# Memory attention with a third buffer of weighed memories and shorter GpSimd steps, and the bias of the ternary layer added by VectorE tile by tile

## The chip, the cores and the metric

The kernel runs on one core of a Trainium2 chip. The time is the device time of one execution in microseconds, and a version is judged by the median of its runs. Engines are called PE (TensorE), PEld (its weight loads), DVE (VectorE), ACT (ScalarE) and POOL (GpSimd), as the profile calls them. Each engine works through its own queue in order; semaphores tie the queues together.

## The reference, cut to what matters

The input x has 8 sequences of 1024 positions with 256 channels. Six residual layers follow one another, each on a layer norm of x:

```python
x = x + 0.5 * fp4_ffn(ln(x))          # block-quantized, hidden 704
x = x + decay_attention(ln(x))        # 16 heads, a scan with a decaying state
x = x + 0.5 * fp4_ffn(ln(x))
x = x + 0.5 * ternary_ffn(ln(x))      # hidden 1024, biases b1 and b2
x = x + memory_attention(ln(x))       # 16 heads of 16
x = x + 0.5 * ternary_ffn(ln(x))
```

The change touches the last three. The ternary layer is `gelu(h @ W1.T + b1) @ W2.T + b2` with weights rounded to -1, 0 and 1. The memory attention is, per head,

```python
q, k, v = h @ Wq.T, h @ Wk.T, h @ Wv.T
sq, sk = elu(q) + 1, elu(k) + 1
rel   = sq . memory_norms[m]                       # for each of 4 memories m
mem   = sum_m softmax_m(mean_s rel) * (sq @ memories[m]) / max(rel, 1e-6)
num   = sq @ cumsum(sk (x) v);  den = max(sq . cumsum(sk), 1e-6)
out   = sigmoid(gate) * mem + (1 - sigmoid(gate)) * num / den
y     = concat_heads(out) @ Wo.T
```

## The kernel before

x stays in SBUF all the time, as 16 groups `X[g]` of 4 tiles of 128 positions x 256 channels (128 x 1024 numbers in fp32 per group, 64 tiles in all). The six layers are stages that run one after another; the statistics of the next layer norm and its first normalized group are begun inside the stage before (`begin`, `ln.advance`).

**The order of the queues.** `pin` chains an instruction behind the last pinned one of the same engine, so in the memory attention PE and DVE run in the order of the source text. POOL's and most of ACT's instructions are not pinned; the scheduler of the build puts them in their queues. In the ternary stages `loose` is set and the scheduler orders DVE too.

**Ternary stages** (`ffn_ternary`). Turn g of the loop transposes group g (`norm_turn`), multiplies group g-1 by W1 in eight chunks (`hidden`, 8 x 4 matmuls, then Gelu `hf`, a rounded copy `hh` on ACT and the rest `hl = hf - hh` on DVE, L1013), and multiplies group g-2 by W2 (`down`, 64 matmuls into `po`, added to x by DVE at L1035). At the start of `hidden`, POOL adds half of b2 to the whole group in one instruction of 128 x 1024 (L991).

**Memory attention** (`attn_memory`). An opening (`i == 0`) projects two groups and a quarter of the third (`project`, then `elu` on DVE, L1423), forms the running sums of sk (`running_sum`, a DVE scan, L1438; there is one buffer `kc` for each half of the channels), and takes the divisors of the first two groups (`divisors`: matmuls into `pr`, ACT copy to `rt`, POOL clamp at L1467). The next groups are normalized by ACT in two steps (L303, L311), tile by tile. After that iteration i works on four tiles at once, j = i mod 4:

- tile a = i-1: scores (`scored`, PE), `weigh_one` (DVE, L1079, 128 x 512), the state and the factors `rw` (DVE reciprocal of `psd` at L1718, product with the mixing weights `mw` at L1719);
- tile b = i-2: memory products `pmo` (PE), `weigh_memory` (DVE writes `mo`, L1586, four times 128 x 256 from PSUM), then `py` (PE, L1136 and L1154);
- tile c = i-3: `pn` (PE transposes), `y = pn * rw` (DVE, L1744), then four POOL additions of the four memories of `mo` into y (L1751);
- tile d = i-4: `pyt` (PE transposes of y), copied by ACT; tile e = i-5: `po` with wo, added to x by DVE (L1773).

The tile `mo` of 128 x 4 x 2 x 4 x 32 has two buffers, so `mo` of tile b cannot be written before the four additions of tile b-2 are done. `py` shares a PSUM bank with the first quarter of `pmo`, so PE begins `py` after the first `weigh_memory`. DVE's order in one iteration is:

```python
weigh_memory(0); weigh_one(1); weigh_memory(1..3)   # L1586, L1079
running_sum                                        # L1438, every second iteration
ln.advance; rw                                     # L1718, L1719
y                                                  # L1744
weigh_one(2), weigh_one(3), weigh_one(0)           # L1079
x += po; elu                                       # L1773, L1423
```

In iterations with j = 3 PE also runs `divisors` of a group two ahead, and POOL clamps its `rt`, 96 x 512 numbers. In the last 12 iterations nothing is projected any more. Once in 8 iterations a sequence begins, and the mixing weights (`mixing`, a softmax over the memories) are formed on the way: `pl` on PE, `lg` on DVE, and so on.

Of the kernel before, what the change touches and what calls it, by code (L numbers as in the profile page):

```python
# [9 lines left out]
F32 = mybir.dt.float32  # L10
# [7 lines left out]
P = 128  # L18
# [4 lines left out]
G = 4  # L23
# [15 lines left out]
def macaron_kernel(  # L39
# [906 lines left out]
    def ffn_ternary(last, after=None):  # L946
        with ExitStack() as st:
# [10 lines left out]
            def norm(g):  # L958
# [9 lines left out]
                xns[g] = xn  # L968

            def norm_turn(g):  # L970
                xn = xns.pop(g)
                xh = lnp.tile([P, 2, TG], F32R, tag="xh", name="xh")
                xl = lnp.tile([P, 2, TG], F32R, tag="xl", name="xl")
                for k in range(2):
                    pt = ps_t.tile([P, TG], F32, tag="pt", name="pt")
                    for j in range(G):
                        nc.tensor.transpose(
                            pt[:, j * P : (j + 1) * P], xn[:, j, k * P : (k + 1) * P], ident
                        )
                    nc.scalar.copy(xh[:, k, :], pt)  # L980
                    pin(
                        nc.vector.tensor_tensor(
                            xl[:, k, :], pt, xh[:, k, :].bitcast(F32), ALU.subtract
                        )
                    )
                xts[g] = (xh, xl)

            def hidden(g, between):

                pin(  # L990
                    nc.gpsimd.tensor_tensor(  # L991
                        X[g], X[g], b2h[:, None, :].to_broadcast([P, G, D]), ALU.add
                    )
                )
                xh, xl = xts.pop(g)
                hh = hp.tile([P, NF, TG], F32R, tag="hh", name="hh")
                hl = hp.tile([P, NF, TG], F32R, tag="hl", name="hl")
                for f in range(NF):
# [18 lines left out]
                    if f < len(between):  # L1017
                        between[f]()
                hs[g] = (hh, hl)

# [344 lines left out]
    def attn_memory(after):  # L1365
        with ExitStack() as st:
# [81 lines left out]
            def divisors(g, pr):  # L1448
# [17 lines left out]
                nc.scalar.activation(rt, pr[0 : NR + 32, :], AF.Identity, accum_out=su)  # L1466
                nc.gpsimd.tensor_scalar(rt, rt, EPS, 1.0, ALU.max, ALU.mult)  # L1467
                sums[g] = su
                proj[g] = (xt, sq, sk, rt)

            def weigh(b):
# [15 lines left out]
                def turned(pl):  # L1487
                    pin(
                        nc.tensor.matmul(pl, lhsT=sb, rhs=ident[:NR, :NR], start=True, stop=True)
                    )  # L1490
                    pin(nc.vector.tensor_scalar(lg, pl, 1.0 / S, None, ALU.mult))

# [100 lines left out]

            n = NG * G
            held = {}
            for i in range(n + 5):
# [3 lines left out]
                if i == 0:  # L1600

                    waiting = []
                    for u in range(min(GB + 1, NG)):
                        norm_turn(u, (2, 3), False)
                        if u < GB and u + 1 < NG:
                            xns[u + 1] = xn_pool.tile([P, G, D], F32, tag="xn", name="xn")
                        for v in range(G if u < GB else 1):
                            pp = ps_s.tile([P, TG], F32, tag="sc", name="pq" if v % 2 else "pk")
                            waiting.append((project(u, v // 2, v % 2 == 1, pp), u, v))
                            if u < GB and u + 1 < NG:  # L1610
                                ln.normalize(xns[u + 1], u + 1, v)
                            if len(waiting) > 1 or u == GB:
                                elu, *at_ = waiting.pop(0)
                                elu()
                                if at_[1] % 2 == 0:
                                    running_sum(at_[0], at_[1] // 2)
                        if u:
                            if waiting and waiting[0][1] == u - 1:
                                waiting.pop(0)[0]()
                            divisors(u - 1, bank(0, [P, TG], "pr"))  # L1620
                    for elu, *at_ in waiting:
# [5 lines left out]
                    if NG == GB:  # L1627
                        divisors(NG - 1, bank(0, [P, TG], "pr"))

# [5 lines left out]
                if 0 <= b < n:  # L1635
                    vz_b, ats_b, before_b, rw_b = chunk[b]
                    mo = cp.tile([P, 4, 2, NM, 2 * HD], F32, tag="mo", name="mo")

# [27 lines left out]
                for r in (1, 2, 3):  # L1666
                    weigh_memory(r)

                if 0 <= b < n:
# [16 lines left out]
                if divide:  # L1686
                    divisors(t, bank(3, [P, TG], "pr"))

# [52 lines left out]
                if 0 <= c < n:  # L1741
# [7 lines left out]
                    yv = y.rearrange("p (c r e) i -> p c r (e i)", c=2, e=2)  # L1749
                    for m in range(NM):  # L1750
                        nc.gpsimd.tensor_tensor(  # L1751
                            yv, yv, mo_c[:, :, :, m, :].rearrange("p r c n -> p c r n"), ALU.add
                        )
                    ys[c] = y
                weigh_one(2)
                weigh_one(3)
                last = t + 1 if j == 3 else t
                elu = None
                if i < n and last < NG:
                    m, of_q = (j + 1) % 4 // 2, j % 2 == 0  # L1760
                    elu = project(last, m, of_q, bank(2, [P, TG], "pq" if of_q else "pk"))
                    if not of_q:
                        held["sum"] = (last, m)
                weigh_one(0)
                if 0 <= a < n:
                    chunk[a] = (vz, [ats[r] for r in range(4)], before, rw)

                def output():
# [3 lines left out]
                    xe = X[e // G][:, e % G, :]  # L1772
                    pin(nc.vector.tensor_tensor(xe, po, xe, ALU.add))  # L1773


                if elu and 0 <= e < n:
                    output()
                if i < n and i % CB == 0:
                    mixing[1](bank(0, [P, NR], "pl"))
                if i < n and j == 2 and t + 1 < NG:  # L1780
# [5 lines left out]
                elif 0 <= e < n:  # L1786
                    output()
                if i < n and i % CB == 0:
# [64 lines left out]
```

## Time and profile before

| | us |
|---|---|
| median of 3 runs | 2725.47 (2719.73 to 2725.5) |
| the profiled execution | 2724.19 |
| its span, from the first to the last instruction | 2722.5 |
| PE busy | 2597.9 (95%) |
| DVE busy | 2088.3 (77%) |
| ACT busy | 1344.6 (49%) |
| POOL busy | 906.4 (33%) |
| L1013, DVE `hl`, 256 times | 210.9 |
| L991, POOL bias, 32 times | 78.3 |
| L1751, POOL additions into y, 256 times | 186.6 |
| L1586, DVE `mo`, 256 times | 95.8 |
| L1467, POOL clamp, 16 times | 31.6 |

The first ternary stage lies between about 1575 and 1847 us of the span, the memory attention between 1847 and 2455 us (its opening to 1880 us, its drain from 2441 us), the second ternary stage from there to the end. A line of the timeline gives the start, the time taken, the engine, the source line, the operation, what it writes and reads, the shape and the count; in square brackets stands how long the engine had been idle, and what released it. Instructions of one line that follow each other are drawn together, and the first and the last then span the time given. A busy share is an average over stages with different limits.

### The profile page before, as it was taken

Reading aid. Unit: us, or ns where it says so; the run is one execution under the profiler, and the core shown is the slowest. Engines: PE = TensorE matmul, PEld = TensorE weight load, DVE = VectorE, ACT = ScalarE, POOL = GpSimd, SP = SyncE. Lnnn points to the kernel's source line nnn. Section 1 sums busy time; section 2 is a strip of 40 time slices with the busy share of each in tenths; the row PEclk is TensorE's granted clock in tenths of the full one; section 3 lists DMA queues with packets and bytes.
Section 4 is the critical chain, followed back from the end, with each engine's and each line's share of the span. In section 5 each row is a group of like instructions: output and inputs, shape, how many; then the busy total and the mean of one; then the engine's idle time right before and its main releaser. Section 6 shows DMA issues by size and latency. Waiting matters only on the chain.

```text
span 2722.5 us, 52848 instructions
## 1 busy us (share of the span) xinstructions
PE 2597.9 (95%) x21270; PEld 1957.1 (72%) x21270; DVE 2088.3 (77%) x4669; ACT 1344.6 (49%) x2932; POOL 906.4 (33%) x817
## 2 busy tenths in 40 slices
PE   5899999999999998999999989999999999989999
PEld 3677777766666666777777778995666666667898
DVE  7888888858777678787878789755888877879775
ACT  5444444443333333444444456666555555436665
POOL 5444445421101003444444421102444444441110
PEclk9999999999999999999999999999999999999999
DMA  6000000000000000000000000000000000000011
GB/s 194 16 1 16 1 1 1 1 1 2 2 2 2 2 2 1 1 1 1 1 1 1 1 1 1 1 1 1 2 2 2 2 2 2 2 2 16 32 39 40
DMA packets 25877, 27.00 MB, mean 10 GB/s; under 512 B 4736, under 2 KB 24736, under 8 KB 25632
## 3 DMA queue, kind: packets, MB, share of 16 engines
q1 hardware_dynamic: 24688, 22.43, 2.6%
q8 instruction: 167, 2.74, 0.4%
q0 software_dynamic: 240, 0.54, 0.1%
q14 instruction: 78, 0.64, 0.1%
q10 hardware_dynamic: 704, 0.66, 0.1%
HBM read 15.23 MB, written 8.39 MB: 9 GB/s over the span
## 4 chain that ended last, share of the span: by engine, by line
PE 70%; DVE 16%; POOL 7%; issue 3%; ACT 2%; DMA 1%; SPq 0%; ACTq 0%; POOLq 0%; DVEq 0%
PE po L839 11%; PE pu L801 9%; PE pg L801 9%; PE po L1027 7%; PE ph L1002 7%; POOL y L1751 5%; PE py L1154 4%; PE sc L1070 3%; PE pk L1168 3%; PE pq L1168 3%; PE po L1168 3%; PE pkv L1168 3%; DVE hl L1013 2%; DVE ln_s L232 2%; PE py L1136 2%
## 5 line engine op out<-in xcount | busy, mean ns | idle before, releaser
L839 PE MATMUL po<-wd,ht 128*128 128x256 f32 (+1 forms) x1536 | 356.7, 382 | 6.1 <-DVE x L848 6.0
L801 PE MATMUL pg<-wgu,xt 128*128 128x352 f32 x1024 | 346.6, 460 | 8.8 <-ACT sg L812 8.6
L801 PE MATMUL pu<-wgu,xt 128*128 128x352 f32 x1024 | 347.3, 462 | 3.0 <-DVE h L814 3.0
L839 PEld LDWEIGHTS po<-wd,ht 128*128 128x128 f32 (+1 forms) x1536 | 283.7, 191 | 44.3 <-DVE x L848 9.0
L772 POOL TENSOR_TENSOR h<-h,q_sc 128x704 f32<-128x704 f32 x128 | 177.6, 1387 | 374.8 <-DVE h L769 370.9
L812 ACT ACTIVATE sg<-pg 128x352 f32<-128x352 f32 x256 | 117.8, 460 | 319.9 <-PE pg L801 319.6
L801 PEld LDWEIGHTS pu<-wgu,xt 128*128 128x128 f32 x1024 | 192.8, 191 | 106.8 <-DVE h L814 5.0
L801 PEld LDWEIGHTS pg<-wgu,xt 128*128 128x128 f32 x1024 | 193.8, 190 | 100.6 <-ACT sg L812 11.9
L1027 PE MATMUL po<-w,hh 128*128 128x256 f32 x1024 | 244.9, 281 | 9.1 <-DVE x L1035 9.1
L1027 PE MATMUL po<-w,hl 128*128 128x256 f32 x1024 | 245.1, 281 | 5.1 <-DVE hl L1013 5.1
L769 DVE SCALAR_TENSOR_TENSOR h<-qp,h 128x704 f32<-128x704 f32 x256 | 227.2, 887 | 20.0 <-ACT qp L765 15.5
L1013 DVE TENSOR_TENSOR hl<-hf,hh 128x512 fp32r<-128x512 f32 x256 | 210.9, 856 | 37.6 <-ACT hh L1011 34.0
L814 DVE TENSOR_TENSOR h<-sg,pu 128x352 f32<-128x352 f32 x256 | 129.5, 515 | 138.3 <-PE pu L801 103.5
L1751 POOL TENSOR_TENSOR y<-y,mo 128x256 f32<-128x256 f32 x256 | 186.6, 729 | 106.9 <-DVE y L1744 91.9
L1002 PE MATMUL ph<-xh,w 128*128 128x512 f32 x512 | 206.5, 405 | 0.9 <-DVE x L1773 0.5
L1002 PE MATMUL ph<-xl,w 128*128 128x512 f32 x512 | 204.3, 400 | 0.0
L991 POOL TENSOR_TENSOR x<-x,b2h 128x1024 f32<-128x1024 f32 x32 | 78.3, 2446 | 375.4 <-DVE xn L963 344.3
L1027 PEld LDWEIGHTS po<-w,hh 128*128 128x128 f32 x1024 | 192.9, 188 | 13.1 <-DVE x L1035 10.8
L758 POOL TENSOR_TENSOR h<-h,q_rs 128x704 f32<-128x704 f32 x128 | 177.7, 1388 | 71.3 <-DVE q_rs L754 59.3
L1027 PEld LDWEIGHTS po<-w,hl 128*128 128x128 f32 x1024 | 193.1, 189 | 7.7 <-DVE hl L1013 5.5
L1010 ACT ACTIVATE hf<-ph,b1c 128x512 f32<-128x512 f32 x256 | 168.5, 695 | 26.0 <-PE ph L1002 17.7
L1079 DVE TENSOR_TENSOR at<-sc,dec 128x512 f32<-128x512 f32 x256 | 158.5, 681 | 17.2 <-PE sc L1070 17.1
(248 smaller groups left out, 5571.4 us busy)
## 6 DMA issues: line engine op xcount, KB each, us to landing
x<-in_x SPq DMA_DIRECT2D x15, 512.0 KB, 8.9
out<-x SPq DMA_DIRECT2D x15, 512.0 KB, 2.9
raw_w<-in_w_t SPq DMA_DIRECT2D x2, 1024.0 KB, 5.3
wqkv<-in_wqkv_t SPq DMA_DIRECT2D x1, 768.0 KB, 6.3
wd_n<-in_w_down SPq DMA_DIRECT2D x1, 704.0 KB, 7.3
w_n<-in_w_up ACTq DMA_DIRECT2D x2, 256.0 KB, 6.6
w_n<-in_w_gate SPq DMA_DIRECT2D x2, 256.0 KB, 5.5
x<-in_x POOLq DMA_DIRECT2D x1, 512.0 KB, 6.0
```

The lines of the kernel that those rows point to most:

```text
L758: nc.gpsimd.tensor_tensor(vb, vb, rs[:, :, None].to_broadcast([P, nb, 16]), ALU.mult)
L769: pin(nc.vector.scalar_tensor_tensor(v, mg, FP4_LEAST, v, ALU.max, op))
L772: nc.gpsimd.tensor_tensor(vb, vb, sc[:, :, None].to_broadcast(list(vb.shape)), ALU.mult)
L801: nc.tensor.matmul(ps, lhsT=xts[g][:, k, j * P : (j + 1) * P], rhs=wgu[:, k, (2 * q + of_up) * NHALF : (2 * q + of_up + 1) * NHALF], start ...
L839: nc.tensor.matmul(po, lhsT=ht[:kn, c, :], rhs=wd[:kn, c, :], start=(c == 0), stop=(c == len(DCH) - 1),)
L1002: nc.tensor.matmul(ph, lhsT=w1[:, k, f * P : (f + 1) * P], rhs=xt[:, k, :], start=(k == 0 and xt is xh), stop=(k == 1 and xt is xl),)
L1010: nc.scalar.activation(hf, ph, AF.Gelu, bias=b1c[:, f : f + 1])
L1013: nc.vector.tensor_tensor(hl[:, f, :], hf, hh[:, f, :].bitcast(F32), ALU.subtract)
L1027: nc.tensor.matmul(po, lhsT=ht[:, f, j * P : (j + 1) * P], rhs=w2[:, f, :], start=(f == 0 and ht is hh), stop=(f == NF - 1 and ht is hl),)
L1079: nc.vector.tensor_tensor(at, sc.rearrange("p m (e t) -> p (m e) t", e=2), weight, ALU.mult)
L1168: nc.tensor.matmul(dst, lhsT=lhsT, rhs=rhs, start=n == 0, stop=n == len(parts) - 1)
L1751: nc.gpsimd.tensor_tensor(yv, yv, mo_c[:, :, :, m, :].rearrange("p r c n -> p c r n"), ALU.add)
```

## The change

1. `mo` gets a third buffer. Three of the four POOL additions move: directly behind the fourth `weigh_memory` POOL adds memories 1, 2 and 3 of tile b into memory 0, in place. Behind y only one addition is left, y + memory 0. For the last three tiles DVE does it.
2. The clamp of `rt` is cut into four pieces of 96 x 128. The source runs one piece in each iteration behind the addition into y; POOL's queue is ordered by the scheduler.
3. In the opening the normalizations are done by DVE in one step (as in the ternary stages, L963) instead of two steps on ACT, and the second running sum of a group is moved behind the transposes of the next group.
4. At the beginning of a sequence `lg` comes ahead of `weigh_one(0)` and not behind the addition to x; the addition to x stays behind `weigh_one(0)`.
5. In the ternary stages the bias is added by DVE, 128 x 256 at a time, behind each of the last four `hl` of `hidden`, where no other work is placed between.

```diff
+            def biased(j, g):
+                xj = X[g][:, j, :]
+                pin(nc.vector.tensor_tensor(xj, xj, b2h, ALU.add))
...
             def hidden(g, between):
-                pin(
-                    nc.gpsimd.tensor_tensor(
-                        X[g], X[g], b2h[:, None, :].to_broadcast([P, G, D]), ALU.add
-                    )
-                )
...
                     if f < len(between):
                         between[f]()
+                    elif f >= NF - G:
+                        biased(f - NF + G, g)
...
                 nc.scalar.activation(rt, pr[0 : NR + 32, :], AF.Identity, accum_out=su)
-                nc.gpsimd.tensor_scalar(rt, rt, EPS, 1.0, ALU.max, ALU.mult)
...
+                def clamp(j):
+                    v = rt[:, j * P : (j + 1) * P]
+                    nc.gpsimd.tensor_scalar(v, v, EPS, 1.0, ALU.max, ALU.mult)
+                return [lambda j=j: clamp(j) for j in range(G)]
...
-                    pin(nc.vector.tensor_scalar(lg, pl, 1.0 / S, None, ALU.mult))
+                    return lambda: pin(nc.vector.tensor_scalar(lg, pl, 1.0 / S, None, ALU.mult))
...
                             if u < GB and u + 1 < NG:
-                                ln.normalize(xns[u + 1], u + 1, v)
+                                nv = G * (u + 1) + v
+                                pin(
+                                    nc.vector.tensor_scalar(
+                                        xns[u + 1][:, v, :], X[u + 1][:, v, :],
+                                        ln.mv[:, nv, 0:1], ln.lr[:, nv : nv + 1],
+                                        ALU.subtract, ALU.mult,
+                                    )
+                                )
...
-                                if at_[1] % 2 == 0:
+                                if at_ == [u, 2]:
+                                    late.append((u, 1))
+                                elif at_[1] % 2 == 0:
                                     running_sum(at_[0], at_[1] // 2)
...
-                    mo = cp.tile([P, 4, 2, NM, 2 * HD], F32, tag="mo", name="mo")
+                    mo = cp.tile([P, 4, 2, NM, 2 * HD], F32, tag="mo", name="mo", bufs=3)
...
                 for r in (1, 2, 3):
                     weigh_memory(r)
+                if 0 <= b < n:
+                    for m in range(1, NM):
+                        nc.gpsimd.tensor_tensor(
+                            mo[:, :, :, 0, :], mo[:, :, :, 0, :], mo[:, :, :, m, :], ALU.add
+                        )
...
-                    for m in range(NM):
-                        nc.gpsimd.tensor_tensor(
-                            yv, yv, mo_c[:, :, :, m, :].rearrange("p r c n -> p c r n"), ALU.add
-                        )
+                    mo_c = mo_c[:, :, :, 0, :].rearrange("p r c n -> p c r n")
+                    if c < n - 3:
+                        nc.gpsimd.tensor_tensor(yv, yv, mo_c, ALU.add)
+                    else:
+                        pin(nc.vector.tensor_tensor(yv, yv, mo_c, ALU.add))
                     ys[c] = y
+                if clamps:
+                    clamps.pop(0)()
...
-                weigh_one(0)
...
+                added = None
                 if elu and 0 <= e < n:
-                    output()
+                    added = output()
                 if i < n and i % CB == 0:
-                    mixing[1](bank(0, [P, NR], "pl"))
+                    mixing[1](bank(0, [P, NR], "pl"))()
+                weigh_one(0)
+                if added:
+                    added()
```

More of the change, by code (lines that the diff above doesn't have):

```diff
@@ L1594, in attn_memory @@
             n = NG * G
+            clamps = []
             held = {}
@@ L1600, in attn_memory @@
                 if i == 0:
-                    waiting = []
+                    waiting, late = [], []
                     for u in range(min(GB + 1, NG)):
                         norm_turn(u, (2, 3), False)
+                        while late:
+                            running_sum(*late.pop(0))
                         if u < GB and u + 1 < NG:
@@ L1619, in attn_memory @@
                                 waiting.pop(0)[0]()
-                            divisors(u - 1, bank(0, [P, TG], "pr"))
+                            clamps += divisors(u - 1, bank(0, [P, TG], "pr"))
                     for elu, *at_ in waiting:
@@ L1627, in attn_memory @@
                     if NG == GB:
-                        divisors(NG - 1, bank(0, [P, TG], "pr"))
+                        clamps += divisors(NG - 1, bank(0, [P, TG], "pr"))
+                    while clamps:
+                        clamps.pop(0)()
                 scs, pmos, ats = {}, {}, {}
@@ L1686, in attn_memory @@
                 if divide:
-                    divisors(t, bank(3, [P, TG], "pr"))
+                    clamps += divisors(t, bank(3, [P, TG], "pr"))
                 if 0 <= a < n:
@@ L1749, in attn_memory @@
                     yv = y.rearrange("p (c r e) i -> p c r (e i)", c=2, e=2)
-                    for m in range(NM):
-                        nc.gpsimd.tensor_tensor(
-                            yv, yv, mo_c[:, :, :, m, :].rearrange("p r c n -> p c r n"), ALU.add
-                        )
+                    mo_c = mo_c[:, :, :, 0, :].rearrange("p r c n -> p c r n")
[3 more added lines that the diff above has]
+                        pin(nc.vector.tensor_tensor(yv, yv, mo_c, ALU.add))
                     ys[c] = y
+                if clamps:
+                    clamps.pop(0)()
                 weigh_one(2)
@@ L1763, in attn_memory @@
                         held["sum"] = (last, m)
-                weigh_one(0)
                 if 0 <= a < n:
-                    chunk[a] = (vz, [ats[r] for r in range(4)], before, rw)
+                    chunk[a] = (vz, ats, before, rw)
                 def output():
@@ L1772, in output @@
                     xe = X[e // G][:, e % G, :]
-                    pin(nc.vector.tensor_tensor(xe, po, xe, ALU.add))
+                    return lambda: pin(nc.vector.tensor_tensor(xe, po, xe, ALU.add))
+                added = None
                 if elu and 0 <= e < n:
-                    output()
+                    added = output()
                 if i < n and i % CB == 0:
-                    mixing[1](bank(0, [P, NR], "pl"))
+                    mixing[1](bank(0, [P, NR], "pl"))()
+                weigh_one(0)
+                if added:
+                    added()
                 if i < n and j == 2 and t + 1 < NG:
@@ L1786, in attn_memory @@
                 elif 0 <= e < n:
-                    output()
+                    output()()
                 if i < n and i % CB == 0:
```

## The prediction

> **What bounds the kernel now.** First the page: PE is busy for 95% of the span, so only time in which PE stands still, or runs at a lower clock, can be won. Then the waits, for two stretches of the memory attention, then the timeline at the places that they name, and the granted clock.
>
> The loop of the memory attention with projections (1880 to 2360 us), columns: total us, times, longest us:
>
> ```profile
> DVE mo L1586 <- POOL y L1751: 35.6, 40, 1.5
> ...
> PE py L1136 <- DVE mo L1586: 12.5, 18, 1.1
> ...
> PE pmo L1573 <- DVE lg L1491: 2.4, 4, 0.6
> ```
>
> The same for the end of the loop, without projections (2360 to 2441 us):
>
> ```profile
> PE py L1136 <- DVE mo L1586: 6.4, 8, 1.4
> ...
> PE py L1154 <- DVE mo L1586: 0.7, 1, 0.7
> ```
>
> So a chain runs from POOL's four additions over the first `mo` of DVE to PE's `py`. The timeline (PE, DVE and POOL alone) shows it in the turn from j = 3 to j = 0:
>
> ```profile
> 2296.04 1.92 POOL L1467 TENSOR_SCALAR rt<-rt 96x512 f32<-96x512 f32 x1 [5.14 <-ACT rt L1466]
> ...
> 2297.02 0.24 DVE L1719 TENSOR_TENSOR rw<-rw,mw 128x80 f32<-128x80 f32 x1
> ...
> 2298.31 3.15 POOL L1751 TENSOR_TENSOR y<-y,mo 128x256 f32<-128x256 f32 x4
> ...
> 2301.50 0.42 DVE L1586 TENSOR_TENSOR mo<-pmo,rw 128x256 f32<-128x256 f32 x1 [1.18 <-POOL y L1751]
> ...
> 2301.98 0.64 PE L1136 MATMUL py<-sq,state 32*32 32x128 f32 x16 [0.88 <-DVE mo L1586]
> ```
>
> POOL clamps 1.92 us, adds 3.15 us, DVE waits 1.18 us for the buffer and PE 0.88 us for DVE. In the drain PE waits for POOL itself:
>
> ```profile
> 2442.18 3.13 POOL L1751 TENSOR_TENSOR y<-y,mo 128x256 f32<-128x256 f32 x4 [3.69 <-DVE y L1744]
> ...
> 2445.36 0.69 PE L1732 MATMUL pyt<-ident,y 128*128 128x128 f32 x2 [2.64 <-POOL y L1751]
> ...
> 2447.02 3.13 POOL L1751 TENSOR_TENSOR y<-y,mo 128x256 f32<-128x256 f32 x4 [1.71 <-DVE y L1744]
> ...
> 2450.20 0.44 PE L1732 MATMUL pyt<-ident,y 128*128 128x128 f32 x2 [2.02 <-POOL y L1751]
> ```
>
> At the start of the second ternary stage (the first is alike, at 1593.5 us) DVE's `hl` stands behind POOL's bias, and PE behind `hl`:
>
> ```profile
> 2468.96 2.34 POOL L991 TENSOR_TENSOR x<-x,b2h 128x1024 f32<-128x1024 f32 x1 [9.39 <-DVE xn L963]
> ...
> 2469.61 2.24 DVE L1013 TENSOR_TENSOR hl<-hf,hh 128x512 fp32r<-128x512 f32 x1
> ...
> 2471.90 0.47 PE L1027 MATMUL po<-w,hl 128*128 128x256 f32 x1 [2.53 <-DVE hl L1013]
> ```
>
> This is the second mechanism of the case: a DVE instruction with both inputs in SBUF does not run while POOL runs an addition. Of 256 `hl`, 27 start under a POOL addition and take 2.33 us, the others 0.68 us. Instructions with an input in PSUM (L1079, L1586) take the same in both cases.
>
> **The change, part by part.** The sum is made against the profiled execution (2724.2 us); the median stands 1.3 us above it.
>
> *Loop.* With a third buffer `mo` never waits for additions: tile b then needs those of tile b-3, done two iterations before. PE's waits are 12.5 + 0.2 us. Most are the 0.8 to 0.9 us of j = 3 to 0, once in 35.1 us; there DVE is ready at 2300.3 us (the `elu` before it is done) and `pmo` ends at 2301.1, so PE goes on without a gap. The small ones (0.2 us, j = 1 to 2) I do not count: DVE's own order leaves only 0.2 us there. I take 11.5 us.
>
> What is moved may cost more than the waits. Three additions (0.8 us each by 3.15/4) now run straight behind the fourth `mo`, from 0.1 to 2.4 us after it, while DVE comes to the scan L1438 (1.2 us, both inputs in SBUF, every second iteration) and to L1719. The scan stands directly behind `mo` in DVE's own queue, POOL starts 0.08 us after a release (2405.42 to 2405.50): the scan goes first and POOL waits. L1719 (0.24 us) can be held for what is left of one addition, 0 to 0.73 us; a DVE instruction held under additions in a row went at the end of the running one (L252 at 2399.85 us: 0.39 us, the addition under it ended 0.36 us on). In j = 1 it costs up to 0.7 us; DVE then stood idle 0.54 us before `mo`, and PE 0.2 us of slack behind it: about 0. Behind L1719 queue y, three `weigh_one`, x and `elu`, on which nothing waits but the next `mo`.
>
> POOL: the built order puts the four clamps together, behind the three additions and ahead of the state and the one addition into y. They last about what the one did (1.92 us; with three more starts perhaps 2.2). y is then complete at about 2.1 us earlier than before, 4 us before `pyt`: hidden. Whether a clamp holds L1719 is seen above: 0.24 us under a running clamp, as in the 14 other cases of it, so 0. The Trainium skill, "SBUF — State Buffer", section "Who interferes with whom", says that a VectorE instruction with two SBUF inputs contends with any GpSimd instruction that reads SBUF, for the whole instruction. By that L1719 would have waited 0.93 us under every clamp, and cutting it in four would win up to 0.4 us of DVE in each of 14 turns; the rows say no, and for the additions they agree.
>
> *`lg` ahead.* The 2.4 us that PE waits for `lg` in the turns to a new sequence end, since `lg` comes one `weigh_one` (0.60 us) sooner; but the next `mo` then has only 0.26 us left before PE waits for it. I take 1.0 us (0 to 2.4).
>
> *End of the loop.* Here PE waits 7.1 us, in steps of 0.73 in a period of 7.62 us, of which PE works 6.89. Without POOL DVE's own round binds: `mo` 0.34, `weigh_one` 0.60, three `mo` 1.07, then the reciprocal at 3.08 us after the first `mo` (it waits for PE and ACT), +0.69, L1719, y 0.33, three `weigh_one` 1.80, x 0.33, a share of the layer norm 0.45. If L1719 (arriving at 3.77 us) is held to the end of the third addition (4.43), the round is 7.5 us; if it slips ahead, 6.9. I take held: 0.25 us in 9 turns, 2.3 us (0 to 6.6).
>
> *Drain.* y 2441.7 to 2442.1, DVE's addition (0.42, perhaps held to 2442.4 by the last POOL sum) to 2442.8, `pyt` and `pn` to 2443.6, y and addition to 2444.4, `pyt` and the copy to 2445.2, `po` of two tiles with x between (0.42 each) to 2448.1, where x ended at 2454.6 before: 6.5 us (5 to 7.5).
>
> *Opening.* DVE gets 8 normalizations (0.41 us, L963) and ACT loses 16 instructions of 0.50. Laid along the queues, the first products of the second group end 1.2 us sooner (DVE's copy no longer stands behind a 1.5 us scan). The next scan still waits for PE's read of the only `kc`, so the normalizations behind it in DVE's queue hold the transposes of the third group 0.6 us longer than before; DVE's next copy is then 1.3 us sooner, and the last product ends 2.4 us sooner. I take 2.4 us (-1.5, if POOL's product L1430 of 1.28 us holds a normalization, to 6).
>
> *Bias.* Removed are 27 holds of 1.65 us, 44.6 us of DVE; added are 128 additions. No row has that form; between 0.24 us for 80 columns (L1719) and 0.68 for 512 (`hl`) it is 0.42 us, 0.34 as the queue advances: 43 to 54 us. So DVE's work stays, but the single holds of 2.3 us go. In a ternary stage DVE is busy for 206 of 272 us, and late only in the first five groups, where PE waits 5.3 and 3.7 us for x (L1035); these stay. The two waits of 2.5 us for `hl` shrink to about 1.5, since two bias additions now stand ahead: 2.0 us (-9, all added work on the path, to 6).
>
> *Clock.* Six stretches here ran at half clock; two of them by the windows view (stretch, its length, busy us of PE, PEld, DVE, ACT, POOL, then PEclk):
>
> ```profile
> 1905.41:1908.82 3.41, 3.41 (x66) 2.82 (x67) 3.20 (x7) 0.37 (x1) 0.00 (x0) 0.50 0.00 0
> ...
> 2472.02:2475.43 3.41, 3.41 (x12) 3.02 (x13) 3.41 (x8) 3.38 (x7) 0.00 (x0) 0.50 0.00 0
> ```
>
> They follow PE waits of 1.1 and 2.5 us that shrink or end; with 1594.8 (6.8 us) and 1871.3 (3.4) that is 17 us at half, 8.5 us at most. I take 3.0 (0 to 8.5). The Trainium skill, "TensorE: Matmul & The Clock Gate", section "Why this matters for your kernels", has the clock fall only after gaps above some 3 us; by it this term is 0 and the sum 25.7. The row after 1.1 us speaks against it.
>
> Sum: 11.5 + 1.0 + 2.3 + 6.5 + 2.4 + 2.0 + 3.0 = 28.7 us. 2724.2 - 28.7 = 2695.5, and 1.3 for the median: 2697.
>
> **The rivals.** (1) The gaps are refilled: `mo` still comes late, now behind L1719 and DVE's order, and the loop wins nothing: 2697 + 11.5 + 2.3 = 2711. For it: the slack of 0.2 us at j = 1. Against: at j = 0 DVE had 1.18 us to spare. (2) The bias binds: DVE is late in the first groups and 9 us more lie on the path, 2697 + 2 + 9 = 2708. Against: equal DVE time. (3) Slower: POOL takes SBUF first and keeps it through its three additions, so the scan starts 2.4 us late in 32 iterations. It decides from about 1.0 us, DVE's slack at j = 2: 32 x 1.4 = 45 us, 2697 + 45 = 2742. Against it are the queue order and L252 above. (4) Nothing to see: DVE is late everywhere, and of all terms only half of the drain is left, 2697 + 28.7 - 3.2 = 2722. For it: DVE is busy for 28.3 of the 35.1 us of four iterations, more than any engine but PE.
>
> **How the numbers follow.** Forecast 0.72, (1) 0.10, (2) 0.07, (3) 0.06, (4) 0.05. A measurement tells about 0.2%, 5.4 us, from no change: faster is below 2720. (1) and (2) are faster too: 0.89; same 0.05; slower 0.06. The range goes down by the upper ends of the end of the loop (4.3 us more), the opening (3.6), the bias (4) and half of the clock's (2.8), 15 us in all, and upwards over (1) and (2) and the lower ends of bias and opening short of both together: 2682 to 2716.
>
> **What the profile after would show.** Right: no wait of `mo` for an addition; `py` waits of j = 0 gone, 35.1 us for four iterations becoming 34.2; `hl` at 0.68 us throughout; no 2 us `pyt` wait. The memory attention, 608 us from 1847 to 2455, takes 608 - 23.7 = 584. Wrong: L1438 at 2 us and more, L1719 with a mean above 0.6, or PE's waits for x (L1035) above 15 us.

## The result, and the profile after

The changed kernel takes 2694.4 us in the median (2692.6 to 2695.3, four runs), the kernel before 2724.7 in the same comparison (2719.7 to 2725.5): a ratio of 0.989, with a 95% interval of 0.9875 to 0.9909. The forecast was 2697. The profiled execution took 2692.6 us, 31.6 less than the one of before; its span is 2690.6 us, 31.9 less. The page first: every engine's busy time, and the engines' shares of the chain that ended last:

```profile
PE 2593.7 (96%) x21270; PEld 1959.1 (73%) x21270; DVE 2107.2 (78%) x4808; ACT 1334.8 (50%) x2916; POOL 857.6 (32%) x830
...
PE 83%; DVE 12%; ACT 2%; POOL 1%; issue 1%; DMA 0%; ACTq 0%; POOLq 0%; DVEq 0%
```

In the kernel before, that last line was:

```profile
PE 70%; DVE 16%; POOL 7%; issue 3%; ACT 2%; DMA 1%; SPq 0%; ACTq 0%; POOLq 0%; DVEq 0%
```

POOL's share of the chain fell from 7% to 1%. But the places where the time was won are not those of the sum. The table cuts both spans at the same PE instructions (the first `ph` and last `po` of a ternary stage, the first `sc`, the last `pq` or `pk`, the last `pmo`, the last `po` of the memory attention):

| stage | before, us | after, us | difference | forecast without the clock's 3.0 |
|---|---|---|---|---|
| all ahead of the first ternary stage | 1580.2 | 1579.3 | -0.9 | 0 |
| first ternary stage | 266.4 | 256.7 | -9.7 | bias, both stages: -2.0 |
| opening of the memory attention | 33.4 | 31.4 | -2.0 | -2.4 |
| its loop with projections | 477.1 | 472.1 | -5.0 | loop and `lg`: -12.5 |
| its end without projections | 81.4 | 80.2 | -1.2 | -2.3 |
| drain | 15.7 | 9.9 | -5.8 | -6.5 |
| second ternary stage | 264.4 | 257.1 | -7.3 | |

The bias, for which 2.0 us were set down, brought 17.0; the loop, for which 12.5 were, brought 5.0. Two errors of opposite sign nearly cancel.

What was announced of single lines did come. All 256 `hl` now take 0.69 us (0.70 at most). In the turn from j = 3 to 0 `mo` waits for no addition, and the clamp in four pieces holds nothing (timeline; POOL, DVE):

```profile
2209.30 2.73 POOL L1473 TENSOR_SCALAR rt<-rt 96x128 f32<-96x128 f32 x4 [0.71 <-ACT rt L1467]
...
2210.29 0.24 DVE L1745 TENSOR_TENSOR rw<-rw,mw 128x80 f32<-128x80 f32 x1
...
2212.39 0.73 POOL L1778 TENSOR_TENSOR y<-y,mo 128x256 f32<-128x256 f32 x1
...
2213.51 0.41 DVE L1592 TENSOR_TENSOR mo<-pmo,rw 128x256 f32<-128x256 f32 x1
```

In the drain the two waits of PE for POOL are gone, since behind y only one addition is left:

```profile
2423.63 0.42 DVE L1770 TENSOR_TENSOR y<-pn,rw 128x256 f32<-128x256 f32 x1 [2.89 <-PE pn L1762]
2424.15 0.42 DVE L1780 TENSOR_TENSOR y<-y,mo 128x256 f32<-128x256 f32 x1
...
2424.73 0.41 PE L1758 MATMUL pyt<-ident,y 128*128 128x128 f32 x2
...
2426.49 0.41 PE L1758 MATMUL pyt<-ident,y 128*128 128x128 f32 x2 [0.27 <-DVE y L1780]
```

In the first ternary stage PE no longer waits for x. These were PE's largest waits there before (total us, times, longest); in the changed kernel only 0.9 us for `hl`, 0.6 for `xn` and 0.4 for `xh` are left:

```profile
PE po L1027 <- DVE x L1035: 5.3, 5, 1.5
...
PE po L1027 <- DVE hl L1013: 2.5, 1, 2.5
```

The loop has new waits of PE, 10.4 us together:

```profile
PE py L1137 <- DVE mo L1592: 6.2, 6, 1.0
PE po L1169 <- DVE rw L1744: 4.2, 5, 1.2
```

The timeline at one of the first kind shows where they come from. The addition into y is short now, so POOL is idle when `sq` is done, and its product `kc` starts 0.01 us ahead of the subtraction of the maximum from `lg`:

```profile
2222.26 1.27 POOL L1431 TENSOR_TENSOR kc<-sq,kc 128x512 f32<-128x512 f32 x1 [2.19 <-DVE mx L1502]
2222.27 1.33 DVE L1507 TENSOR_TENSOR lg<-lg,mx 128x64 f32<-128x64 f32 x1
2223.53 0.41 DVE L1592 TENSOR_TENSOR mo<-pmo,rw 128x256 f32<-128x256 f32 x1
...
2223.99 0.64 PE L1137 MATMUL py<-sq,state 32*32 32x128 f32 x16 [1.04 <-DVE mo L1592]
```

And at one of the second kind: the sums ahead of y now run where DVE has the layer norm's small instructions and the reciprocal behind them:

```profile
2179.57 1.28 DVE L1439 TENSOR_TENSOR_SCAN kc<-ones,carry,sk 128x512 f32<-128x512 f32 x1
2179.73 3.29 POOL L1691 TENSOR_TENSOR mo<-mo 128x256 f32<-128x256 f32 x3 [2.54 <-DVE mo L1592]
...
2180.76 0.64 DVE L252 SCALAR_TENSOR_TENSOR ln_h<-ln_r,ln_va 128x16 f32<-128x16 f32 x1
...
2181.64 0.59 DVE L254 SCALAR_TENSOR_TENSOR ln_r<-ln_h,ln_r 128x16 f32<-128x16 f32 x1
...
2183.25 0.64 DVE L1744 RECIPROCAL rw<-psd 128x80 f32<-128x80 f32 x1
...
2183.95 0.92 PE L1169 MATMUL po<-wo,yt 128*128 128x256 f32 x3 [1.22 <-DVE rw L1744]
```

Instructions of 0.17 us take 0.6. The scan goes first, as forecast, and POOL's first sum waits for it: in all 27 turns with a scan that sum takes 1.57 to 1.64 us in place of 0.72, so the three end some 0.9 us later and reach further into what stands behind the scan.

Over the loop DVE is busy for 407.3 us, before for 386.1, with 911 instructions both times (windows view; columns as in the prediction; before, then after):

```profile
1879.96:2357.02 477.06, 456.88 (x6164) 320.89 (x6164) 386.06 (x911) 261.56 (x671) 223.34 (x306) 1.00 0.01 2
1867.36:2339.44 472.08, 456.95 (x6164) 323.40 (x6164) 407.32 (x911) 260.21 (x671) 257.25 (x351) 1.00 0.01 2
```

So two theories went into the experiments. *Loop:* the third buffer is worth what was forecast or more, and the sums ahead of y take part of it back; against it, that DVE's order refills the gaps whatever POOL does. *Ternary stages:* the holds of `hl` (the time that an `hl` waits under POOL's bias) cost them 17 us; against it, that the gain came from the build's scheduler, which deals out the layer norm's statistics more thinly when DVE has the bias to add (41 and 42 of them in the fourth and fifth group before, 17 and 29 after).

### The profile page after: what moved, and what is told of

It is laid out like the page before. It is cut to its first block, busy times and chain, and to the rows that moved or that the text cites. A ratio compares the mean times of both kernels' runs of the same rounds, so it can differ in the third digit from the quotient of the medians.

```text
span 2690.6 us, 52938 instructions
## 1 busy us (share of the span) xinstructions
PE 2593.7 (96%) x21270; PEld 1959.1 (73%) x21270; DVE 2107.2 (78%) x4808; ACT 1334.8 (50%) x2916; POOL 857.6 (32%) x830
## 4 chain that ended last, share of the span: by engine, by line
PE 83%; DVE 12%; ACT 2%; POOL 1%; issue 1%; DMA 0%; ACTq 0%; POOLq 0%; DVEq 0%
PE po L839 11%; PE pu L801 10%; PE pg L801 10%; PE po L1028 9%; PE ph L1001 8%; PE py L1155 4%; PE sc L1071 4%; PE pk L1169 4%; PE po L1169 4%; PE pkv L1169 4%; PE pq L1169 3%; PE py L1137 2%; PE pt L824 2%; DVE at L1080 2%; PE pmo L1579 1%; DVE h L769 1%
## 5 line engine op out<-in xcount | busy, mean ns | idle before, releaser
L801 PEld LDWEIGHTS pg<-wgu,xt 128*128 128x128 f32 x1024 | 193.8, 190 | 99.3 <-ACT sg L812 11.5
L1691 POOL TENSOR_TENSOR mo<-mo 128x256 f32<-128x256 f32 x192 | 164.2, 855 | 183.4 <-DVE mo L1592 170.0
L1012 DVE TENSOR_TENSOR hl<-hf,hh 128x512 fp32r<-128x512 f32 x256 | 168.6, 686 | 39.4 <-ACT hh L1010 35.9
L1080 DVE TENSOR_TENSOR at<-sc,dec 128x512 f32<-128x512 f32 x256 | 158.7, 683 | 17.2 <-PE sc L1071 17.1
L1080 DVE TENSOR_TENSOR at<-sc,tri 128x512 f32<-128x512 f32 x256 | 164.2, 679 | 0.5 <-PE sc L1071 0.5
## 6 DMA issues: line engine op xcount, KB each, us to landing
w_n<-in_w_gate SPq DMA_DIRECT2D x2, 256.0 KB, 5.3
w_n<-in_w_up ACTq DMA_DIRECT2D x2, 256.0 KB, 6.4
```

The lines of the kernel that those rows point to most:

```text
L801: nc.tensor.matmul(ps, lhsT=xts[g][:, k, j * P : (j + 1) * P], rhs=wgu[:, k, (2 * q + of_up) * NHALF : (2 * q + of_up + 1) * NHALF], start ...
L1012: nc.vector.tensor_tensor(hl[:, f, :], hf, hh[:, f, :].bitcast(F32), ALU.subtract)
L1080: nc.vector.tensor_tensor(at, sc.rearrange("p m (e t) -> p (m e) t", e=2), weight, ALU.mult)
L1691: nc.gpsimd.tensor_tensor(mo[:, :, :, 0, :], mo[:, :, :, 0, :], mo[:, :, :, m, :], ALU.add)
```

## The experiments

Each was timed in three rounds beside the kernel before, whose median was 2723.4 to 2724.9. Diffs are against the changed kernel, unless something else is said.

**The third buffer alone**, against the kernel before:

```diff
-                    mo = cp.tile([P, 4, 2, NM, 2 * HD], F32, tag="mo", name="mo")
+                    mo = cp.tile([P, 4, 2, NM, 2 * HD], F32, tag="mo", name="mo", bufs=3)
```

> The kernel before with a third buffer of mo and nothing else: POOL's four additions stay behind y. The loop went from 477.1 to 472.1 us in the full change, where the prediction had 11.5 us from PE's waits plus 1.0 from lg. Theory A: those waits were worth what the prediction said, and the sums moved ahead of y took part of it back, because small DVE instructions (lg at L1507 1.33 us after and 0.30 before, the product L1745 0.29 and 0.24, the layer norm's 0.58 and 0.17) now fall under a POOL instruction. Then the buffer alone gives a loop of 464 to 468 us, its end below 79 us, the small instructions keep their durations of before, and the time is 2709 to 2713 us. Theory B: PE's waits were refilled by DVE's own order whatever POOL does. Then the loop is 472 us or more and the time 2716 to 2721 us.

Measured: 2703.5 us, ratio 0.992 (0.9908 to 0.9941). The loop takes 458.1 us, 19.0 less than before and 14.0 less than in the changed kernel; its end 79.0. No wait of PE for `mo` is left in the loop's list.

```profile
1881.53:2339.62 458.09, 451.92 (x6164) 319.71 (x6164) 385.19 (x910) 261.13 (x671) 223.16 (x306) 1.00 0.01 2
```

Theory A, and by more than it said. The small instructions, in the changed kernel's loop (groups by line: out<-in, count, busy us, mean ns, idle before):

```profile
L1745 DVE TENSOR_TENSOR rw<-rw,mw 128x80 f32<-128x80 f32 x54 | 19.0, 353 | 1.9
L1507 DVE TENSOR_TENSOR lg<-lg,mx 128x64 f32<-128x64 f32 x6 | 8.0, 1330 | 0.2
L253 DVE TENSOR_TENSOR ln_h<-ln_h,ln_r 128x16 f32<-128x16 f32 (+1 forms) x9 | 4.2, 464 | 0.3
```

and here, with the additions behind y:

```profile
L1719 DVE TENSOR_TENSOR rw<-rw,mw 128x80 f32<-128x80 f32 x54 | 13.1, 242 | 1.9
L1501 DVE TENSOR_TENSOR lg<-lg,mx 128x64 f32<-128x64 f32 x7 | 2.0, 288 | 0.2
...
L253 DVE TENSOR_TENSOR ln_h<-ln_h,ln_r 128x16 f32<-128x16 f32 (+1 forms) x9 | 1.6, 174 | 0.3
```

Behind y DVE works on `at`, `y` and `x`, which have an input in PSUM; there an addition of POOL holds nothing (`at` takes 0.68 us under one and 0.68 without, `x` 0.41 in both kernels).

**Additions behind y in the changed kernel** (in the loop only; the last three tiles keep sums and DVE's addition):

```diff
-                if 0 <= b < n:
+                if n - 3 <= b < n:
...
-                    mo_c = mo_c[:, :, :, 0, :].rearrange("p r c n -> p c r n")
+                    mo_cs = [mo_c[:, :, :, m, :].rearrange("p r c n -> p c r n") for m in range(NM)]
                     if c < n - 3:
-                        nc.gpsimd.tensor_tensor(yv, yv, mo_c, ALU.add)
+                        for m in range(NM):
+                            nc.gpsimd.tensor_tensor(yv, yv, mo_cs[m], ALU.add)
                     else:
-                        pin(nc.vector.tensor_tensor(yv, yv, mo_c, ALU.add))
+                        pin(nc.vector.tensor_tensor(yv, yv, mo_cs[0], ALU.add))
```

> The changed kernel with its three sums undone in the loop: POOL adds the four memories onto y behind y, as before, into three buffers; the sums ahead of y and VectorE's addition stay for the last three tiles. The buffer alone gave a loop of 458.1 us, the changed kernel 472.1. Theory A (the sums ahead of y hold the small DVE instructions that stand there, and free POOL for its product kc, which holds lg): the loop is 456 to 460 us, L1745 back to 0.24 us and lg to 0.30, the drain stays at 10 us, and the time is 2677 to 2684 us. Theory B (lg ahead or the clamp in pieces cost the 14 us): the loop stays at 468 us or more and the time at 2689 us or more.

Measured: 2679.4 us, ratio 0.984 (0.9826 to 0.9855). The loop takes 459.2 us, its end 78.2, the drain 8.8, and DVE's busy time in the loop is back at 388.2:

```profile
1870.50:2329.70 459.20, 453.90 (x6164) 321.56 (x6164) 388.23 (x912) 260.38 (x671) 231.51 (x347) 1.00 0.01 2
```

Theory A. This version beats both kernels: of the change, the step that moves the sums costs 12.9 us in the loop. L1745 is back at 0.24 us; the subtraction `lg` fell from 1.33 to 0.62 us only, not to the 0.30 expected.

**The maximum ahead of `sq`**, sums still ahead of y:

```diff
-                    nc.scalar.activation(lg, lg, AF.Exp)
+                    return lambda: nc.scalar.activation(lg, lg, AF.Exp)
...
+                exp = mixing[2]() if i < n and i % CB == 0 else None
                 if elu:
                     elu()
...
-                if i < n and i % CB == 0:
-                    mixing[2]()
+                if exp:
+                    exp()
```

> The changed kernel, sums ahead of y, with one move: in the turns to a new sequence the maximum and its subtraction from lg stand ahead of sq in DVE's order, so that POOL's product kc, which sq releases, can no longer start 0.02 us ahead of the subtraction. PE waited 6.3 us in all for mo in these turns, 1.04 us each. Theory A (the hold of lg, 1.03 us once in each of these turns, is what PE waits for): lg takes 0.30 us, PE's waits of py shrink to under 2 us, the loop is 465 to 468 us, and the time is 2687 to 2691 us. Theory B (mo is late by DVE's own order, the hold is covered): loop 471 to 473 us, time 2692 to 2697 us.

Measured: 2689.6 us, ratio 0.988 (0.9863 to 0.9893), loop 467.1. `lg` takes 0.23 us, and the 6.2 us of waits for `mo` have left the list; the 4.2 for `rw` (here 4.4) stay:

```profile
L1507 DVE TENSOR_TENSOR lg<-lg,mx 128x64 f32<-128x64 f32 x6 | 1.3, 225 | 0.2
```

Theory A: 5.0 of the 12.9 us are this one instruction, held once in each of these turns. For the other 7.9 the layer norm's terms, L1745 and the like are what is left; no run parts them.

**Both edits:**

> Both of these edits together: additions behind y in the loop, and the maximum ahead of sq. With the additions behind y POOL is busy until after lg, so lg is not held there, and the move should bring little. Theory A: within 2 us of the kernel with the additions behind y alone, 2677 to 2684 us. Theory B: the two holds are independent, and this one is 3 us or more below it.

Measured: 2679.0 us, ratio 0.984 (0.9821 to 0.9854), loop 459.4: as with the additions behind y alone.

**Two buffers in the changed kernel:**

```diff
-                    mo = cp.tile([P, 4, 2, NM, 2 * HD], F32, tag="mo", name="mo", bufs=3)
+                    mo = cp.tile([P, 4, 2, NM, 2 * HD], F32, tag="mo", name="mo")
```

> The changed kernel with two buffers of mo in place of three. With the sums ahead of y the buffer that mo takes is free when the one addition of the last iteration is done, some 2.4 us sooner than the four of before. Theory A: that is early enough, mo waits for nothing, and the third buffer is idle here: 2692 to 2697 us, loop 472 us. Theory B: mo still comes to a buffer that is not free in the turns from j = 3 to 0, where four clamps stand ahead of that addition: 0.5 to 1 us in 14 turns, 2700 to 2708 us.

Measured: 2693.5 us, ratio 0.989 (0.9876 to 0.9906), loop 472.3. Theory A: third buffer and sums ahead are two cures for one wait. With the second the first is idle, and the second is the dearer one (loops of 472.3 and 458.1 us).

**Bias on POOL again:**

```diff
+                pin(nc.gpsimd.tensor_tensor(
+                    X[g], X[g], b2h[:, None, :].to_broadcast([P, G, D]), ALU.add))
                 xh, xl = xts.pop(g)
...
-                    elif f >= NF - G:
-                        biased(f - NF + G, g)
```

> The changed kernel with the ternary bias back on POOL, one addition for a group at the head of its turn. The ternary stages took 266.4 and 264.4 us before and 256.7 and 257.1 us after. Theory A (the bias made all of this): they return to 266 and 264 us and the time is 2709 to 2713 us. The prediction's term was 2.0 us and at most some 3 us of clock: 2697 to 2700 us. If the stages gained because what comes ahead of them ends differently (another state of the queues, another clock), they stay near 257 us and the time is below 2700 us.

Measured: 2708.5 us, ratio 0.994 (0.9929 to 0.9959); the stages take 266.5 and 262.9 us. Theory A, 14.1 us in the median. The second stage does not return quite to its 264.4: in the kernel before a stretch at half clock that begins in the drain reaches 3.7 us into it (1.9 us at most), and here none does.

**Bias on POOL, statistics kept in their turn** (against the kernel with the bias on POOL; the first call is shortened):

```diff
+            if anchor:      # in pin: issue behind the second hl of the turn
+                tc.add_manual_dep(ins.ins, anchor[0].name, NoSync, reason="order")
...
+                        if f == 1:
+                            anchor.append(low.ins)      # low: the hl just issued
                         between[f]()
+                        anchor.clear()
```

> The same, bias back on POOL, but each turn's share of the layer norm's statistics is kept in DVE's order behind the second hl of its turn, so that they are not dealt out ahead of it: 10 to 14 a group from the third group to the ninth, where the kernel before has 41 and 42 in the fourth and fifth (the changed kernel has 17 and 29). The holds of hl by POOL stay. Theory A (the order of the statistics made the gain: DVE is full only where they stand densely): the stages take 256 to 258 us as in the changed kernel although hl is held for 2.3 us once in a group, and the time is 2692 to 2697 us. Theory B (the holds of hl cost the time wherever they fall): the stages stay above 262 us and the time is 2706 to 2713 us.

Measured: 2717.9 us, ratio 0.998 (0.997 to 0.9989), stages of 269.2 and 266.7, above both theories' ranges. The theory of the statistics' order, mine at that point, falls: with 10 of them in a group PE waits for x in more groups of the first stage (eight, where the kernel with the bias on POOL has five), not in fewer. The timeline shows where. In this group, as in most, POOL's bias meets the second `hl`, which takes 2.33 us; the first x of the group stands behind the other six `hl` in DVE's queue, and PE waits for it with 10 statistics between:

```profile
1667.15 2.41 POOL L1003 TENSOR_TENSOR x<-x,b2h 128x1024 f32<-128x1024 f32 x1 [14.27 <-DVE xn L971]
...
1667.77 2.33 DVE L1025 TENSOR_TENSOR hl<-hf,hh 128x512 fp32r<-128x512 f32 x1 [0.70 <-ACT hh L1023]
...
1675.38 0.41 DVE L1050 SCALAR_TENSOR_TENSOR x<-po,x 128x256 f32<-128x256 f32 x1
...
1675.85 0.39 PE L1042 MATMUL po<-w,hh 128*128 128x256 f32 x1 [0.91 <-DVE x L1050]
...
1678.04 0.42 DVE L1050 SCALAR_TENSOR_TENSOR x<-po,x 128x256 f32<-128x256 f32 x1 [1.32 <-PE po L1042]
```

Soon after, DVE itself stands idle for 1.32 us. It is not short of time in the group; it is late in the stretch from the second `hl` to the first x, and hold and statistics together use up what that stretch has to spare. In the kernel before, the groups of the first stage came every 17.1 to 17.7 us where statistics stood densely in them, and every 15.9 where none did, though nearly all of them have an `hl` of 2.33 us. So the hold alone costs nothing there; the next run takes the holds away and leaves the statistics.

**Bias left out:**

```diff
-                    elif f >= NF - G:
-                        biased(f - NF + G, g)
```

> The changed kernel with the ternary bias b2 left out altogether. No hold of hl, no addition for the bias, and the statistics dealt out densely, 41 and 42 in the fourth and fifth group, as in the kernel before. Theory A (DVE full): in these groups DVE has 17.2 us of work per group before; without 1.65 us of hold it is 15.5, below PE's 15.9, so the stages take 256 to 258 us and the time is 2692 to 2696 us. Theory B (the dense order alone costs it, holds or not): the stages stay above 261 us and the time above 2702 us.

Measured: 2691.7 us, ratio 0.988 (0.9868 to 0.9897), stages 256.0 and 256.2, with the statistics as dense as before. The groups with statistics now come every 15.9 or 16.0 us, like those without. Theory A: without the holds the dense order costs nothing; only both together do. DVE's 128 additions cost 2.7 us in the median (2694.4 - 2691.7).

**The same tiles on POOL:**

```diff
-                pin(nc.vector.tensor_tensor(xj, xj, b2h, ALU.add))
+                pin(nc.gpsimd.tensor_tensor(xj, xj, b2h, ALU.add))
```

> The changed kernel with the same 128 bias additions of 256 columns, but issued to POOL. One POOL addition of this size takes 0.73 us, so an hl that meets one is held for 0.7 us at most and not for 1.65. Bias on POOL in one piece gave 2708.5 us, no bias 2691.7, on DVE in tiles 2694.4. Theory A (what costs is the hold between the second hl and the first x of a group, and four short additions in a row hold several hl in turn): the sum of the holds is as large as before, the stages take 263 to 267 us and the time is 2703 to 2709 us. Theory B (the tiles are what helps, and not the engine): the stages take 257 to 260 us and the time is 2694 to 2699 us.

Measured: 2706.5 us, ratio 0.994 (0.9925 to 0.9954), stages 263.0 and 263.9. Theory A: the engine matters, not the tiles. Mean `hl` in the changed kernel, with the bias on POOL in one piece, and in tiles:

```profile
L1012 DVE TENSOR_TENSOR hl<-hf,hh 128x512 fp32r<-128x512 f32 x256 | 168.6, 686 | 39.4 <-ACT hh L1010 35.9
```

```profile
L1017 DVE TENSOR_TENSOR hl<-hf,hh 128x512 fp32r<-128x512 f32 x256 | 210.9, 856 | 37.7 <-ACT hh L1015 34.0
```

```profile
L1012 DVE TENSOR_TENSOR hl<-hf,hh 128x512 fp32r<-128x512 f32 x256 | 190.3, 771 | 42.3 <-ACT hh L1010 38.6
```

In tiles half of the hold of `hl` stays (21.7 us of 42.3), and 38 normalizations `xn` take 0.82 us in place of 0.40, another 16 us, so that nearly as much time is held as in one piece.

**Opening and last additions undone:**

```diff
-                                pin(nc.vector.tensor_scalar(xns[u + 1][:, v, :], ...))
+                                ln.normalize(xns[u + 1], u + 1, v)
...
-                    if c < n - 3:
-                        nc.gpsimd.tensor_tensor(yv, yv, mo_c, ALU.add)
-                    else:
-                        pin(nc.vector.tensor_tensor(yv, yv, mo_c, ALU.add))
+                    nc.gpsimd.tensor_tensor(yv, yv, mo_c, ALU.add)
```

> The changed kernel with the opening and the drain undone: the normalizations of the opening back on ACT, with running_sum in its old place, and the one addition of the last three tiles back on POOL. The two lie in stages of their own. By the prediction's terms (2.4 and 6.5 us) the time rises to 2703 us; by the stages of the two traces (opening 33.4 to 31.4 us, drain 15.7 to 9.9) by 2.0 and at most 5.8: 2700 to 2703 us. The drain's part should be smaller, since three of its four additions stay ahead of y: one POOL addition of 0.73 us in place of one by DVE of 0.42, in three tiles, 1 to 2 us, which gives 2696 to 2699 us. Theory B (neither counts, the stages moved because of what comes ahead of them): 2692 to 2695 us.

Measured: 2694.1 us, ratio 0.989 (0.9878 to 0.9908): no change. The opening takes 32.7 us in place of 31.4, the drain 9.4 in place of 9.9 (with the third buffer alone 16.0). The sums ahead made the drain short; who does the last addition does not matter. The opening's 1.3 us are below what the time can tell.

**The clamp in one piece** (`divisors` issues it whole and returns no pieces):

> The changed kernel with the clamp in one piece. In the changed kernel's trace the four pieces stand together in POOL's order, behind the three sums, and take 2.73 us against 1.92 in one piece. Theory A (the prediction's): the clamp holds no DVE instruction and y is early enough either way: 2692 to 2696 us. Theory B (a clamp in one piece stands ahead of the sums or of the state in a turn, and y comes later): 0.5 us or more in 14 turns, above 2700 us.

Measured: 2694.2 us, ratio 0.989 (0.9873 to 0.9906), loop 472.1: nothing, as forecast.

**`lg` back behind the fourth `weigh_one` and x:**

```diff
+                weigh_one(0)
                 if elu and 0 <= e < n:
-                    added = output()
+                    output()()
                 if i < n and i % CB == 0:
                     mixing[1](bank(0, [P, NR], "pl"))()
-                weigh_one(0)
-                if added:
-                    added()
```

> The changed kernel with lg back behind the fourth weigh_one and x. The prediction's term was 1.0 us (0 to 2.4): 2694 to 2697 us. In the kernel before, PE waited 2.4 us for lg in these turns; in the changed one that wait is gone, and PE waits 6.3 us for mo behind the held subtraction. Theory A (two waits in the same turns, one behind the other, so that lg ahead gained nothing): loop 472 to 474 us, time 2693 to 2697 us. Theory B (both waits then stand): 2697 to 2700 us.

Measured: 2694.0 us, ratio 0.989 (0.9877 to 0.9907), loop 472.1. PE's wait of `pmo` for `lg` is back (3.4 us), that of `py` for `mo` is shorter (4.3 in place of 6.2), and the loop takes as long: theory A.

## Why the prediction was right, and where it was not

The time lay 2.6 us under the forecast and inside the range, and that it came so near is luck: in the spans the bias brought 15.0 us more than was set down, and against it the loop brought 7.5 less, the other three stages of the memory attention 2.2 less, and the clock's 3.0 is no term of its own. The chain that the prediction began from (POOL's additions, DVE's `mo`, PE's `py`) was the right one, and the buffer alone shows it. By steps:

- *Loop, 11.5 us.* For the buffer this was too small: 19.0 us. What PE stands still in the loop fell from 20.2 to 6.2 us, and its busy time by 5.0 (456.9 to 451.9), of which the half-clock stretch at 1905 us, gone there, is 1.7 at most; the rest was not followed up.
- *"What is moved may cost more than the waits ... about 0."* This step failed. The sums ahead of y cost 12.9 us in the loop. The prediction followed two instructions that a sum could hold, the scan and L1719, and had both about right (the scan goes first; L1719 rose from 0.24 to 0.35 us). It left out the others that stand in that part of DVE's queue and were held too: the layer norm's terms (0.17 us, held to 0.6), and in the turns to a new sequence `tot`, `sb`, `sm` and `lg`. The row L252 that it quoted for the length of a hold was one of them. It let POOL wait for the scan, but still had the sums end 2.4 us behind `mo`; they end some 0.9 us later in those turns. And it did not ask what POOL does with the 2.4 us that it wins behind y: it starts `kc` sooner, under `lg`.
- *Clamp, 0.* Right. The "14 other cases" are 14 in all.
- *`lg` ahead, 1.0.* 0: another wait in the same turns came next.
- *End of the loop, 2.3.* 1.2. The prediction's own rounds, 7.62 and 7.5 us, give 0.12 us a turn, 1.1 in 9 turns; its 0.25 does not follow from them. One turn there shows the same mechanism: L1745 and `tot` held to 0.62 us each, PE waiting 2.06 us for `pl`, and behind it 3.41 us at half clock, from 2358.4. With the additions behind y this stage wins 3.2.
- *Drain, 6.5.* 5.8, by the sums; DVE's addition has no part in it.
- *Opening, 2.4.* 2.0 in the trace, of which 1.3 go with the normalizations on DVE and the moved running sum, which were undone together. The kernel before has a half-clock stretch there (1871 us, 1.7 us at most) that the changed one has not.
- *Bias, 2.0.* 17.0. The wrong sentence is that PE's waits for x "stay", because DVE's work stays. The amount of DVE's work nearly stayed (205.0 and 201.3 us in the first stage), the hold's place decided: 1.65 us in the one stretch of a group that PE waits for, against four additions of 0.42 us, each behind another `hl`. Of the 17.0, PE stood still 11.0 us less and was busy for 6.0 less; in the stages of before 14.0 us ran at half clock, 7.0 of the time at most. The lower bound (-9) is a difference of busy times and for the upper (6) no source is given; 17.0 lay outside.
- *Clock, 3.0.* From 1590 us on the kernel before had six stretches at half clock, 27.3 us long (1595, 1871, 1905, 2445, 2452 and 2472); the changed one has two of 3.4 (2358 and 2420). That is 20.5 us less at half speed, 10.2 of the time at most, and it is contained in the stages above. So the term of 3.0 was probably too small. The stretches stand near waits of PE, but not every wait of a length has one (below), and what decides is not shown.

Of the rivals (1) came nearest: the loop was partly refilled, though by POOL's holds and not by DVE's order. (3) had the right resource; DVE was held through one POOL instruction at a time, not through three, and in small instructions. (2) was wrong, 2.7 us for all the additions. The signs set up for "wrong" (L1438 at 2 us, L1719 above 0.6, waits for x) all stayed quiet, because they named the instructions that the prediction had thought of. Those for "right" were missed twice: the memory attention took 593.6 us and not 584, and four iterations of the loop 34.8 and not 34.2.

## What to carry to other kernels

When a POOL step is moved, list every DVE instruction that stands beside its new place, with the operands it reads: between PSUM-reading instructions a POOL addition was free, among short ones with two SBUF inputs, or a TENSOR_SCALAR on SBUF, it multiplied their time. Ask also what POOL starts sooner once it is free. And cost a hold by where it falls between a producer and the engine that waits, not by its share of busy time: 1.65 us a group were free in some groups and cost 1.2 or more in others.

## What the runs showed of the hardware

- Beside POOL additions not only DVE instructions with two SBUF inputs wait. A TENSOR_SCALAR with one tensor input does too: 38 `xn` of 128 x 256 took 0.81 to 0.83 us under POOL's bias tiles, 0.40 alone. In the changed kernel's loop BATCH_NORM_STATS2 (0.40 us in 31 cases under a POOL addition, 0.42 in 16 others), RECIPROCAL of `sm` in SBUF (0.25 in both) and of `psd` in PSUM (0.64 and 0.66), `at`, `mo`, `y` and `x` do not. The Trainium skill, "SBUF — State Buffer", section "Who interferes with whom", counts `tensor_scalar` among the forms that can take the shared port pair, and these rows agree.
- By the same section any GpSimd instruction that reads SBUF would hold a two-input one. POOL's clamp does not: the product with `mw` (L1719, L1745) takes 0.24 us in 14 of 14 cases under it, in one piece and in four, in each of the traces of the two kernels and of the runs with the third buffer alone and the clamp in one piece.
- The wait goes both ways: a sum of POOL that begins under DVE's scan took 1.57 to 1.64 us (27 of 27), 0.72 without; three sums take 2.33 us, and 3.29 where the first met a scan.
- A gap of 2.06 us in PE's work (2354.8 to 2356.8) was followed by 3.41 us at half clock (2358.4), and in the kernel before one of 1.14 us (1904.2 to 1905.4) by the same at 1905.4. But with the bias left out the gap of 2.07 us at the same place was followed by none. With the additions behind y, where no gap behind 1576 us is longer than 1.4 us, the clock stays whole from there to the end of the span. The length of a gap alone does not decide in these runs.
